# Macaron block on one NeuronCore: counts by one scan, other last groups, quarters in two steps, first loads in another order

## The chip, the core and the metric

The kernel runs on one NeuronCore of a Trainium2 chip. The time is the device time of one execution in microseconds. The figure for the kernel before is the median of three runs. Profiles are one execution each, taken by the hardware profiler; in their rows PE is TensorE, PEld its weight loads, DVE is VectorE, ACT is ScalarE, POOL is GpSimd and SP is SyncE, which issues most DMAs.

## What is computed

A block of three residual layers on x of 8 x 1024 rows of 512 numbers (fp32): half a mixture of experts, attention, half a mixture of experts with the same weights.

```python
def moe(x):                                   # T = 8192 tokens, E = 32, C = 320
    logits = xt @ w_router
    probs = softmax(logits); top1 = argmax(probs); gate = probs[top1]
    pos = cumsum(onehot(top1))[t, top1] - 1   # a token's place in its expert's queue
    accepted = pos < C
    slot = where(accepted, top1 * C + pos, E * C)
    buf[slot] = xt
    y = (silu(buf @ w_gate) * (buf @ w_up)) @ w_down
    out_tok = where(accepted, y[slot] * gate, 0)
    return xt + out_tok

x = x + 0.5 * moe(layernorm(x))
x = x + attention(layernorm(x))               # 16 heads of 32, rotary positions
x = x + 0.5 * moe(layernorm(x))
```

## The kernel before, in words

**Stages.** The front (`front`) normalizes all 64 tiles of 128 rows, computes their router logits and gives each token its slot. The first expert stage (`experts`) gathers each expert's rows, multiplies them and writes first_rows. Attention (`Attention`) reads first_rows, writes x2, and in the course of its own work routes the rows for the third layer. The second expert stage writes the output. The instructions of TensorE, ScalarE, VectorE and GpSimd stand in the order in which the Python code emits them, one queue for each engine, and each instruction waits by semaphores for what it needs. SP's queue is put in order by the scheduler of the framework.

**The front.** A loop over tiles (line 423) runs four things at different distances: it loads four tiles at a time (L373), takes the statistics of tile i + 12 on VectorE (L156, L157), normalizes tile i + 2 on ScalarE (L177), transposes tile i on TensorE (L199) and copies the transposed tile into xT (L429). Behind these, generators stand in a list `work`, and `advance` (line 410) runs each of them once per tile up to its next WAIT:

- `scaled` works out the scales of a group of tiles from its statistics. VectorE adds epsilon (L167), POOL raises to -0.5 (L168), and VectorE derives three more rows (L170 to L172).
- `products` turns four tiles' xT into logits: the router products (L234), a copy (L241), a fold (L246), a copy to lg (L251).
- `routed` runs `route` for one group, and waits until the group ahead of it has counted.

The groups have 4, six times 8, and three times 4 tiles (line 361).

**route.** For a group of G tiles it finds each token's largest logit (L285 to L294), writes oh, the one-hot rows as [128, G, 32] (L295), and counts: run holds, for each tile and expert, how many tokens of the earlier tiles went there. run begins with a copy of the carry (L299), and G adds follow, each reading what the one ahead of it wrote (L301). Two products then sum, for each token, the tokens ahead of it in its own tile and those of the tiles ahead (L306, L310). L316 picks the token's own expert out of them; from that come pos (L324), slot (L338) and spare (L343). For each tile POOL issues one indirect DMA (L347) that scatters 128 pairs of token number and gate into the table. The last group's counts go to `sorted` (line 454), which ranks the experts by size: a product (L465), some steps of VectorE, a second product (L479) and the numbers `order` and `arm` (L487 to L492). SP reads order and loads the first expert's weights, 3 MB (L509); all engines read arm and branch to one of four profiles of widths.

**The expert stage.** `places` loads the whole table into slots (L580) and turns it into indices by two small products (L584): the first gives come (which rows to gather, L586) and ids (L587), the second the gates (L587); go (L588, L591) is derived from ids. `gather` (L670) issues three indirect DMAs on POOL for an expert's rows. `begin` normalizes and transposes the first expert's rows. Then, for each of 32 experts, `feed` runs the products gate and up (L755), and down (L797, L805), while it prepares the next one; the expert after that is gathered meanwhile. Experts whose last block has at most 32 rows compute it in quarters; `quarters` (line 599) gives them their own indices: a copy of the table's rows four times over (L610), two products (L618), and come, go and gates from them (L622 to L629). It is called once, ahead of step r = 2.

**The opening of attention.** `opening` (line 1150) loads two weight tiles wqk (L1231, from `load_qk`), the first four tiles of rows xt, the tables cos and sin, and four more tiles of rows (L1164); it takes the statistics and scales tile by tile, transposes, and begins the products pq (L1258). From there TensorE works through scores, exponentials and sums in stages. `finished` (line 1514) normalizes four tiles of the new rows at a time and routes them with the same `route`, in groups of four; the last two groups come behind the last products (L1495).

Of the kernel before, what the change touches and what calls it, by code (L numbers as in the profile page):

```python
# [13 lines left out]
F32 = mybir.dt.float32  # L14
# [3 lines left out]
ALU = mybir.AluOpType  # L18
# [32 lines left out]
class Block:  # L51
# [31 lines left out]
    def constants(self, pool, w_router):  # L83
        nc = self.nc
        self.ident = pool.tile([P, P], F32, name="ident")
        make_identity(nc, self.ident)

        self.before = pool.tile([P, P], F32, name="before")
        make_upper_triangular(nc, self.before, val=1.0, diag=False)
        self.ones = pool.tile([P, P], F32, name="ones")  # L90
        nc.vector.memset(self.ones, 1.0)

        self.rev = pool.tile([P, G, self.E], F32, name="rev")
        nc.gpsimd.iota(
            self.rev, pattern=[[0, G], [-1, self.E]], base=self.E, channel_multiplier=0,
            allow_small_or_imprecise_dtypes=True,
        )

        self.token = pool.tile([P, self.NT], F32, name="token")
        nc.gpsimd.iota(  # L100
            self.token, pattern=[[P, self.NT]], base=0, channel_multiplier=1,
            allow_small_or_imprecise_dtypes=True,
        )
        self.w_router = pool.tile([P, self.KD, self.E], F32, name="w_router")
        nc.sync.dma_start(self.w_router, w_router.rearrange("(k p) e -> p k e", p=P))

        self.fold = pool.tile([P, self.E], F32, name="fold")
        nc.vector.tensor_copy(self.fold, self.ident[:, 0 : self.E])
        for k in range(1, P // self.E):
            nc.vector.tensor_tensor(  # L110
                self.fold, self.fold, self.ident[:, k * self.E : (k + 1) * self.E], ALU.add
            )
        self.power = pool.tile([P, G], F32, name="power")
        nc.vector.memset(self.power, -0.5)

        NS, E, NB = self.NS, self.E, self.NB
        self.past, self.away, self.beyond = (
            pool.tile([P, self.NT], F32, name=name) for name in ("past", "away", "beyond")
        )
        for t, add in (  # L120
            (self.past, NS), (self.away, NS - E * P), (self.beyond, -self.T)
        ):
            nc.vector.tensor_scalar(t, self.token, float(add), None, ALU.add)

        R = NB * E
        self.own = pool.tile([R, E], F32, name="own")
        self.columns = pool.tile([R, R], F32, name="columns")
        self.number = pool.tile([E, 1], F32, name="number")  # L130
        nc.gpsimd.memset(self.columns, -1.0)
        for i in range(NB):
            at = slice(i * E, (i + 1) * E)
            nc.vector.tensor_copy(self.own[at, :], self.ident[at, at])
            nc.vector.tensor_scalar(
                self.columns[at, at], self.rev[at, 0, :], -1.0, float(E), ALU.mult, ALU.add
            )
        nc.gpsimd.iota(
            self.number, pattern=[[0, 1]], base=0, channel_multiplier=1,
            allow_small_or_imprecise_dtypes=True,  # L140
        )
        self.most = pool.tile([1, len(self.profiles) - 1, E], F32, name="most")
        for j, widths in enumerate(self.profiles[:-1]):
            for a, z, width in sorted_steps(widths):
                nc.gpsimd.memset(
                    self.most[:, j, a:z],
                    float((width if width < self.C else self.T) * E + E),
                )

        self.acts = [pool.tile([P, self.KF, self.C], F32, name=f"a{i}") for i in range(2)]  # L150
        for t in self.acts:
            nc.gpsimd.memset(t, 0.0)
# [101 lines left out]
    def route(  # L254
# [22 lines left out]
            return x.unsqueeze(2).to_broadcast([P, G, E])  # L277

        token = self.token[:, t0 : t0 + G]
        ex, oh = wide("ex"), wide("oh")  # L280
        mx, se, m = narrow("mx"), narrow("se"), narrow("m")

        row = pool.tile([P, G, 2], F32, tag="row", bufs=deep, name="row")
# [11 lines left out]
        nc.vector.tensor_tensor(oh, rev, over_e(m), ALU.is_equal)  # L295


        run = pool.tile([P, G + 1, E], F32, tag="run", bufs=2, name="run")
        nc.vector.tensor_copy(run[:, 0, :], carry)  # L299
        for j in range(G):  # L300
            nc.vector.tensor_tensor(run[:, j + 1, :], run[:, j, :], oh[:, j, :], ALU.add)  # L301
        order = counted and counted(run[:, G, :])
        yield WAIT, 1
        yield PE, 1.2
        pp = psum.tile([P, G, E], F32, tag=tag, name="pp")
        nc.tensor.matmul(  # L306
            pp.rearrange("p g e -> p (g e)"), self.before,
            oh.rearrange("p g e -> p (g e)"), start=True, stop=False,
        )
        nc.tensor.matmul(  # L310
            pp.rearrange("p g e -> p (g e)"), self.ones,
            run[:, 0:G, :].rearrange("p g e -> p (g e)"), start=False, stop=True,
        )
        if apart:
            yield WAIT, 1
        nc.vector.tensor_tensor(lg, pp, oh, ALU.mult)  # L316
        yield DVE, 1.2
        nc.vector.tensor_reduce(se, ex, AX.X, ALU.add)
        nc.vector.reciprocal(se, se)
# [24 lines left out]
        for j in range(G):  # L344
# [5 lines left out]
                in_=row[:, j, :],  # L350
                in_offset=None,
            )
        return run[:, G, :]

    def front(self, pool, psum, x, rest, spare, carry, table, ranked):

# [1 line left out]


        nc, NT, D, KD, E = self.nc, self.NT, self.D, self.KD, self.E  # L360
        sizes = [G // 2] + [G] * (NT // G - 2) + [G // 2] * 3
        starts = [sum(sizes[:i]) for i in range(len(sizes))]
        group = [g for g, size in enumerate(sizes) for _ in range(size)]
        mv = pool.tile([P, NT, 2], F32, name="mv", bufs=1)
# [148 lines left out]
    def experts(self, table, ranks, src, dst, weights, loaded=None, others=None):  # L513
# [16 lines left out]
        for i in tc.Switch(which, len(self.profiles)):  # L530
            widths = self.profiles[i]
            with (
# [3 lines left out]
                tc.manual_schedule(engines={F.PE, F.Activation, F.DVE, F.Pool}),  # L536
            ):
                expert = Expert(self, (wp, ap, ps), src, views, others)
                expert.places(table, matrix)


                now = expert.gather(0, widths[0])
                now.weights = loaded or self.load(wp, order, 0, weights, hold="wu")
                expert.begin(now)
                following = expert.gather(1, widths[1])
                for r in range(E):
                    if r == 2:
                        expert.quarters(widths)
                    if following:
                        following.weights = self.load(  # L550
                            wp, order, r + 1, weights, hold=None if r else "wg"
# [7 lines left out]
class Expert:  # L559
# [7 lines left out]
    def places(self, table, matrix):  # L567
# [14 lines left out]
        for i, at in enumerate((ids, self.gates)):  # L582
            pt = self.ps.tile([P, R], F32, tag="tp", name="pt")
            nc.tensor.matmul(pt, rows[:, :, i], matrix, start=True, stop=True)  # L584
            if i == 0:
                nc.vector.tensor_scalar(self.come, pt, float(s.T - 1), None, ALU.min)  # L586
            nc.vector.tensor_copy(at, pt)  # L587
        nc.vector.tensor_copy(self.go[:, 0 : R - E], ids[:, 0 : R - E])  # L588
        for i in range(2):
# [9 lines left out]
    def quarters(self, widths):  # L599
# [3 lines left out]
        few = [r for r, width in enumerate(widths) if self.parts(width) == 4]  # L603
        if not few:
            return
        assert few == list(range(few[0], few[-1] + 1)) and few[0] > 3
        last = slice(R - E, R)
        at = slice(R - E + few[0], R - E + few[-1] + 1)
        rows = ap.tile([R, 4, n * 2], F32, tag="four", bufs=1, name="four")
# [3 lines left out]
            .to_broadcast([E, 4, n * 2]),  # L613
        )
        rows = rows.rearrange("r k (s c) -> r (k s) c", c=2)
        for i in range(2):
            pt = self.ps.tile([P, len(few)], F32, tag="tp", name="pt")
            nc.tensor.matmul(  # L618
# [203 lines left out]
class Attention:  # L822
# [327 lines left out]
    def opening(self):  # L1150
# [1 line left out]


        nc, s, pool, psum = self.nc, self.s, self.pool, self.psum
        self.load_qk(0, 0)

        def fetch(half):
            xs = []
# [7 lines left out]
            return xs  # L1166

        xs = [fetch(0)]
        nc.sync.dma_start(self.cs, self.cos)
        nc.sync.dma_start(self.sn, self.sin)  # L1170
        xs.append(fetch(1))
# [526 lines left out]
```

## Time and profile before

| | us |
|---|---|
| median of three runs (4716.10 to 4721.66) | 4720.27 |
| the profiled execution | 4731.47 |
| its span, first to last instruction | 4729.7 |
| front, to the issue of slots (L580) | 0 to 171.8 |
| first expert stage, to the last scatter of its rows | 171.8 to 935.8 |
| attention, to the issue of slots in front of the second stage | 938.3 to 3955.6 |
| second expert stage | 3955.6 to 4729.7 |

The page gives the busy time of each engine over the span: PE 4519.9 us, DVE 2827.4, ACT 2939.7, POOL 789.1. TensorE's granted clock has a mean of 0.979 of full speed.

A line of the timeline gives the start in us, the busy time in us, engine, source line, operation, out<-in by the program's names with partitions x elements, how many instructions were merged (x8), and in brackets the idle time of the engine ahead of it with the instruction that ended it, as far as the profile can tell. Lines of stretches of time give the length, then for PE, PEld, DVE, ACT and POOL the busy us and the number of instructions, then TensorE's granted clock, the share of the DMA engines and GB/s. SPq lines are DMAs that SP issues.

### The profile page before, as it was taken

The page shows a single profiled execution, that of the slowest core. Times are in us where ns is not written, and L with a number is a line of the kernel's source. Part 1 is how long each engine was busy: PE and PEld are TensorE (multiplying, and loading weights), DVE is VectorE, ACT ScalarE, POOL GpSimd, SP SyncE. Part 2 cuts the span into 40 slices and gives each one's busy share as a digit, 9 for nine tenths or more (in the row PEclk, how much of TensorE's full clock was granted, in tenths as well). Part 3 has the DMA queues.
Part 4 walks back from the last instruction along what each step waited for, and adds up shares of the span by engine and source line. Part 5 has one row for each costly group of instructions (what it writes and reads, how often), then busy time and mean ns, then how long its engine had stood idle before and what let it go on. Part 6 is the DMA issues. An engine that isn't in the chain of part 4 may idle for free.

```text
span 4729.7 us, 69515 instructions
## 1 busy us (share of the span) xinstructions
PE 4519.9 (96%) x24896; PEld 2111.9 (45%) x24896; DVE 2827.4 (60%) x5604; ACT 2939.7 (62%) x5886; POOL 789.1 (17%) x806
## 2 busy tenths in 40 slices
PE   6699999898999999999999999999999986999999
PEld 4466777632233333333333333333333324667777
DVE  8434433367667767767777777777776754344333
ACT  6212222169998888888888888888888872111111
POOL 4433333210000000010110110110110002222221
PEclk8799999989999999999999999999999998999999
DMA  4456666511112212212212212212211104455564
GB/s 145 139 185 194 208 208 230 186 56 35 34 32 61 75 37 68 69 41 67 71 40 69 68 44 63 70 44 63 72 46 54 59 26 157 167 172 190 181 207 140
DMA packets 287642, 481.60 MB, mean 102 GB/s; under 512 B 47000, under 2 KB 82274, under 8 KB 287282
## 3 DMA queue, kind: packets, MB, share of 16 engines
q1 hardware_dynamic: 253042, 400.43, 27.3%
q0 software_dynamic: 33952, 76.41, 5.1%
q8 instruction: 198, 3.24, 0.3%
q14 instruction: 162, 1.33, 0.1%
q10 hardware_dynamic: 288, 0.20, 0.0%
HBM read 376.18 MB, written 88.01 MB: 98 GB/s over the span
## 4 chain that ended last, share of the span: by engine, by line
PE 83%; DVE 7%; ACT 4%; issue 3%; DMA 2%; POOL 1%; SPq 0%; DVEq 0%; POOLq 0%; ACTq 0%
PE sa L1379 14%; PE gp L755 10%; PE pq L1258 9%; PE up L755 9%; PE po L1461 9%; PE yp L797 9%; PE sb L1359 6%; PE px L1495 4%; PE pv L1329 4%; PE sb L1386 3%; ACT junk L1398 2%; DVE nm L1394 2%; PE tp L199 2%; PE tp L743 1%; ACT pr L1391 1%
## 5 line engine op out<-in xcount | busy, mean ns | idle before, releaser
L1394 DVE TENSOR_REDUCE nm<-sa 128x2 f32<-128x1024 f32 x1024 | 1248.5, 1220 | 648.5 <-PE sa L1379 387.3
L1398 ACT ACTIVATE junk<-sa,nm 128x512 f32<-128x512 f32 x2048 | 1407.2, 687 | 264.8 <-DVE nm L1394 185.7
L1379 PE MATMUL sa<-k,q 32*128 32x512 f32 x4096 | 1147.5, 642 | 9.7 <-ACT pr L1391 3.5
L1391 ACT ACTIVATE pr<-sb 128x1024 f32<-128x1024 f32 x1024 | 1040.6, 1018 | 108.7 <-PE sb L1386 104.4
L1386 PE MATMUL sb<-q,k 32*128 32x512 f32 x4096 | 1063.9, 603 | 0.0
L760 ACT ACTIVATE sg<-gp 128x320 f32<-128x320 f32 (+7 forms) x256 | 99.5, 389 | 1108.5 <-PE gp L755 1081.1
L1309 POOL TENSOR_TENSOR raw<-raw,a 128x512 f32<-128x512 f32 x126 | 160.6, 1274 | 2367.9 <-DMA rot<-raw 1673.2
L1461 PE MATMUL po<-pr,v 128*32 128x512 f32 x4096 | 549.6, 609 | 0.0
L755 PE MATMUL gp<-bT,wg 128*128 128x272 f32 (+7 forms) x2048 | 510.2, 392 | 0.0
L1258 PE MATMUL pq<-hT,wqk 128*128 128x512 f32 x1024 | 506.7, 619 | 1.0 <-DVE hT L1199 0.8
L755 PE MATMUL up<-bT,wu 128*128 128x272 f32 (+7 forms) x2048 | 503.5, 389 | 0.0
L797 PE MATMUL yp<-wd,a 128*128 128x512 f32 x1024 | 460.3, 592 | 0.0
L1359 PE MATMUL sb<-mrow,ones 3*128 3x512 bf16 x2048 | 393.8, 385 | 41.7 <-ACT pr L1391 40.2
L755 PEld LDWEIGHTS gp<-bT,wg 128*128 128x128 f32 x2048 | 385.2, 191 | 93.9 <-issue 22.6
L755 PEld LDWEIGHTS up<-bT,wu 128*128 128x128 f32 x2048 | 386.6, 190 | 75.4
L1359 PEld LDWEIGHTS <-ones 3*128 3x128 bf16 x2048 | 99.9, 91 | 712.1 <-issue 670.4
L780 DVE TENSOR_TENSOR a<-sg,up 128x320 f32<-128x320 f32 (+7 forms) x256 | 110.6, 432 | 495.1 <-PE up L755 469.0
L1398 ACT ACTIVATION_READ_ACCUMULATOR junk<-sa,nm 128x1 f32 x2048 | 398.2, 194 | 0.0
L1386 PEld LDWEIGHTS sb<-q,k 32*128 32x128 f32 x4096 | 360.4, 184 | 0.1
L1379 PEld LDWEIGHTS sa<-k,q 32*128 32x128 f32 x4096 | 304.8, 183 | 70.3 <-ACT pr L1391 30.2
L1258 PEld LDWEIGHTS pq<-hT,wqk 128*128 128x128 f32 x1024 | 174.8, 189 | 315.8 <-issue 227.0
L801 DVE SCALAR_TENSOR_TENSOR ys<-yp,gates,x 128x512 f32<-128x512 f32 x128 | 96.1, 751 | 337.0 <-PE yp L797 337.0
(199 smaller groups left out, 4222.4 us busy)
## 6 DMA issues: line engine op xcount, KB each, us to landing
wg<-in_w_gate SPq DMA_DIRECT2D x64, 1024.0 KB
wu<-in_w_up SPq DMA_DIRECT2D x64, 1024.0 KB
wd<-in_w_down SPq DMA_DIRECT2D x64, 1024.0 KB
rot<-raw SPq DMA_DIRECT2D x1008, 32.0 KB
all<-in_x SPq DMA_DIRECT2D x32, 512.0 KB
xt<-first_rows SPq DMA_DIRECT2D x64, 256.0 KB
xr<-first_rows SPq DMA_DIRECT2D x64, 256.0 KB
d<-inverse SPq DMA_DIRECT2D x256, 64.0 KB
```

The lines of the kernel that those rows point to most:

```text
L755: nc.tensor.matmul(acc, w[:, k, f * P : (f + 1) * P], to.bT[:, k, 0:width], start=(k == 0), stop=(k == s.KD - 1),)
L797: nc.tensor.matmul(yp, a[:, f, i * P : (i + 1) * P], wd[:, f, :], start=(f == 0), stop=(f == KF - 1),)
L1258: nc.tensor.matmul(acc, w[:, which, k, :], self.hT[b, n][:, k, :], start=(k == 0), stop=(k == KD - 1),)
L1329: nc.tensor.matmul(acc, hT[:, k, at : at + P], self.w_vo[:, k, :], start=(k == 0), stop=(k == KD - 1),)
L1359: nc.tensor.matmul(sb[:, h, :], self.ones16[at : at + 3, :], row[at : at + 3, :], start=True, stop=False,)
L1379: nc.tensor.matmul(sa[:, h, :], qa[at, (g * 4 + j) * P : (g * 4 + j + 1) * P], ka[at, m * 512 : (m + 1) * 512], start=True, stop=True,)
L1386: nc.tensor.matmul(sb[:, h, :], k[at, t * P : (t + 1) * P], q[at, n * 512 : (n + 1) * 512], start=False, stop=True,)
L1391: nc.scalar.activation(pr, sb, AF.Exp)
L1394: nc.vector.tensor_reduce(nm[:, m, j, pair : pair + 2], sa, AX.X, ALU.max, negate=True)
L1398: nc.scalar.activation(self.junk, sa[:, h - pair, :], AF.Exp, bias=nm[:, m, j, h : h + 1], accum_out=se[:, m, j, h : h + 1],)
L1461: nc.tensor.matmul(self.po[at : at + HD, :], self.v[b][t][:, c * P + at : c * P + at + HD], prs[h // 2 * 2][:, h % 2, :], start=(t == 0), ...
L1495: nc.tensor.matmul(acc, self.oT[b, c, half][:, j * P : (j + 1) * P], self.w_vo[:, c, :], start=False, stop=(c == KD - 1),)
```

## The change

- `route` counts by one instruction. oh becomes a view of a tile `taken` of [128, 32, G + 1]: for each expert one column for the carry and then G columns for the tiles. A scan runs over all 32 x (G + 1) elements: each result is the one before it times `going`, plus `taken`. going is a constant with 0 in each expert's first column and 1 elsewhere, so that the sum starts anew with each expert's carry. run, pp and the operands of the two products take the same layout, with the experts outside and the tiles inside; L295 writes oh, and L316 reads pp and oh, through views with the two dimensions exchanged. The tiles going are filled on POOL at the start.
- The groups of the front have 4, seven times 8, and 4 tiles.
- `places` stops behind come; the first expert's gather is emitted there, and the rest of `places` follows.
- `quarters` stops behind its copy. The copy is emitted ahead of step 1, the products and indices ahead of step 3.
- In `opening`, load_qk stands behind the first four tiles of rows.

```diff
--- before.py
+++ after.py
@@ -110,6 +110,12 @@
             nc.vector.tensor_tensor(
                 self.fold, self.fold, self.ident[:, k * self.E : (k + 1) * self.E], ALU.add
             )
+
+        self.going = {}
+        for n in (G // 2, G):
+            self.going[n] = t = pool.tile([P, self.E, n + 1], F32, name=f"going{n}")
+            nc.gpsimd.memset(t, 1.0)
+            nc.gpsimd.memset(t[:, :, 0:1], 0.0)
         self.power = pool.tile([P, G], F32, name="power")
         nc.vector.memset(self.power, -0.5)
 
@@ -277,7 +283,12 @@
             return x.unsqueeze(2).to_broadcast([P, G, E])
 
         token = self.token[:, t0 : t0 + G]
-        ex, oh = wide("ex"), wide("oh")
+        ex = wide("ex")
+
+        taken = pool.tile(
+            [P, E, G + 1], F32, tag=f"oh{G}", bufs=2 if apart else 1, name="oh"
+        )
+        oh = taken[:, :, 1 : G + 1].rearrange("p e g -> p g e")
         mx, se, m = narrow("mx"), narrow("se"), narrow("m")
 
         row = pool.tile([P, G, 2], F32, tag="row", bufs=deep, name="row")
@@ -295,25 +306,24 @@
         nc.vector.tensor_tensor(oh, rev, over_e(m), ALU.is_equal)
 
 
-        run = pool.tile([P, G + 1, E], F32, tag="run", bufs=2, name="run")
-        nc.vector.tensor_copy(run[:, 0, :], carry)
-        for j in range(G):
-            nc.vector.tensor_tensor(run[:, j + 1, :], run[:, j, :], oh[:, j, :], ALU.add)
-        order = counted and counted(run[:, G, :])
+        run = pool.tile([P, E, G + 1], F32, tag=f"run{G}", bufs=2, name="run")
+        nc.vector.tensor_copy(taken[:, :, 0], carry)
+        nc.vector.tensor_tensor_scan(
+            run.rearrange("p e g -> p (e g)"),
+            self.going[G].rearrange("p e g -> p (e g)"),
+            taken.rearrange("p e g -> p (e g)"), 0.0, ALU.mult, ALU.add,
+        )
+        order = counted and counted(run[:, :, G])
         yield WAIT, 1
         yield PE, 1.2
-        pp = psum.tile([P, G, E], F32, tag=tag, name="pp")
+        pp = psum.tile([P, E, G], F32, tag=tag, name="pp")
         nc.tensor.matmul(
-            pp.rearrange("p g e -> p (g e)"), self.before,
-            oh.rearrange("p g e -> p (g e)"), start=True, stop=False,
-        )
-        nc.tensor.matmul(
-            pp.rearrange("p g e -> p (g e)"), self.ones,
-            run[:, 0:G, :].rearrange("p g e -> p (g e)"), start=False, stop=True,
-        )
+            pp, self.before, taken[:, :, 1 : G + 1], start=True, stop=False,
+        )
+        nc.tensor.matmul(pp, self.ones, run[:, :, 0:G], start=False, stop=True)
         if apart:
             yield WAIT, 1
-        nc.vector.tensor_tensor(lg, pp, oh, ALU.mult)
+        nc.vector.tensor_tensor(lg, pp.rearrange("p e g -> p g e"), oh, ALU.mult)
         yield DVE, 1.2
         nc.vector.tensor_reduce(se, ex, AX.X, ALU.add)
         nc.vector.reciprocal(se, se)
@@ -350,7 +360,7 @@
                 in_=row[:, j, :],
                 in_offset=None,
             )
-        return run[:, G, :]
+        return run[:, :, G]
 
     def front(self, pool, psum, x, rest, spare, carry, table, ranked):
 
@@ -358,7 +368,7 @@
 
 
         nc, NT, D, KD, E = self.nc, self.NT, self.D, self.KD, self.E
-        sizes = [G // 2] + [G] * (NT // G - 2) + [G // 2] * 3
+        sizes = [G // 2] + [G] * (NT // G - 1) + [G // 2]
         starts = [sum(sizes[:i]) for i in range(len(sizes))]
         group = [g for g, size in enumerate(sizes) for _ in range(size)]
         mv = pool.tile([P, NT, 2], F32, name="mv", bufs=1)
@@ -536,16 +546,19 @@
                 tc.manual_schedule(engines={F.PE, F.Activation, F.DVE, F.Pool}),
             ):
                 expert = Expert(self, (wp, ap, ps), src, views, others)
-                expert.places(table, matrix)
+                places = expert.places(table, matrix)
+                next(places)
 
 
                 now = expert.gather(0, widths[0])
+                next(places, None)
                 now.weights = loaded or self.load(wp, order, 0, weights, hold="wu")
                 expert.begin(now)
                 following = expert.gather(1, widths[1])
+                quarters = expert.quarters(widths)
                 for r in range(E):
-                    if r == 2:
-                        expert.quarters(widths)
+                    if r in (1, 3):
+                        next(quarters, None)
                     if following:
                         following.weights = self.load(
                             wp, order, r + 1, weights, hold=None if r else "wg"
@@ -584,6 +597,7 @@
             nc.tensor.matmul(pt, rows[:, :, i], matrix, start=True, stop=True)
             if i == 0:
                 nc.vector.tensor_scalar(self.come, pt, float(s.T - 1), None, ALU.min)
+                yield
             nc.vector.tensor_copy(at, pt)
         nc.vector.tensor_copy(self.go[:, 0 : R - E], ids[:, 0 : R - E])
         for i in range(2):
@@ -603,7 +617,7 @@
         few = [r for r, width in enumerate(widths) if self.parts(width) == 4]
         if not few:
             return
-        assert few == list(range(few[0], few[-1] + 1)) and few[0] > 3
+        assert few == list(range(few[0], few[-1] + 1)) and few[0] > 4
         last = slice(R - E, R)
         at = slice(R - E + few[0], R - E + few[-1] + 1)
         rows = ap.tile([R, 4, n * 2], F32, tag="four", bufs=1, name="four")
@@ -613,6 +627,7 @@
             .to_broadcast([E, 4, n * 2]),
         )
         rows = rows.rearrange("r k (s c) -> r (k s) c", c=2)
+        yield
         for i in range(2):
             pt = self.ps.tile([P, len(few)], F32, tag="tp", name="pt")
             nc.tensor.matmul(
@@ -1152,7 +1167,6 @@
 
 
         nc, s, pool, psum = self.nc, self.s, self.pool, self.psum
-        self.load_qk(0, 0)
 
         def fetch(half):
             xs = []
@@ -1166,6 +1180,7 @@
             return xs
 
         xs = [fetch(0)]
+        self.load_qk(0, 0)
         nc.sync.dma_start(self.cs, self.cos)
         nc.sync.dma_start(self.sn, self.sin)
         xs.append(fetch(1))
```

## The prediction

> **What bounds the kernel now.** I read the page first: the busy rows and the chain of waits. The chain is TensorE for 83 % of the span, and nothing in the change removes or shortens a large product. So the change can only move the seams: the front (0 to 172 us), the first steps of each expert stage, and the opening of attention.
>
> ```profile
> PE 83%; DVE 7%; ACT 4%; issue 3%; DMA 2%; POOL 1%; SPq 0%; DVEq 0%; POOLq 0%; ACTq 0%
> ```
>
> Then the busy time by stretches, and the timeline of VectorE, in the front. From 28 to 113 us VectorE paces it: it is busy 17 to 18 of every 20 us, and one group of eight tiles takes 15.76 us (spare at 70.20, the next at 85.96) with one idle stretch of 0.73. ScalarE has 14.5 and POOL 12.8 busy in the same 20.
>
> ```profile
> 60.00:80.00 20.00, 13.65 (x82) 8.81 (x82) 17.96 (x64) 14.50 (x29) 12.75 (x13) 0.83 0.55 150
> 79.16 0.42 DVE L295 TENSOR_TENSOR oh<-rev,m 128x256 f32<-128x256 f32 x1
> 79.50 0.17 DVE L299 COPY run<-run 128x32 f32<-128x32 f32 x1
> 79.71 1.77 DVE L301 TENSOR_TENSOR run<-run,oh 128x32 f32<-128x32 f32 x8
> 81.40 0.69 DVE L156 BATCH_NORM_STATS2 st<-xq 128x6 f32<-128x512 f32 x1
> ```
>
> Behind 113 us the timeline shows another regime. POOL issues one scatter each 1.27 us, and VectorE waits on things that had ended.
>
> ```profile
> 125.06 0.59 PE L310 MATMUL pp<-run,ones 128*128 128x256 f32 x2
> 130.13 0.42 DVE L316 TENSOR_TENSOR lg<-pp,oh 128x256 f32<-128x256 f32 x1 [5.11 <-PE tp L199]
> 146.17 0.29 DVE L316 TENSOR_TENSOR lg<-pp,oh 128x128 f32<-128x128 f32 x1 [3.51 <-remote]
> 160.25 0.39 SPq L509 DMA_DIRECT2D wg<-in_w_gate  x1
> 165.67 0.97 POOL L347 DMA_INDIRECT table<-row,slot  x1 [0.30 <-issue]
> 171.77 0.36 SPq L580 DMA_DIRECT2D slots<-table  x1
> ```
>
> The product that L316 reads ends at 125.65 and at 143.28; VectorE starts 4.5 and 2.9 us later. From 149 to 156 its small steps also lag: from mx to slot the last group takes 12.6 us, where the same twelve rows in front of the second expert stage (3939.6 to 3948.2) take 8.6. That is 4.5 + 2.9 + 4.0 = 11.4 us of stalls, found almost nowhere else in the trace, and the profiled execution (4731.47: span 4729.7 and 1.8 around it) is 11.2 above the median. I take the stalls to belong to the profiled execution. The sum below is made in its times with these stalls taken out, which is the median's frame (4720.27).
>
> **Counts by one scan.** Per group of eight it removes the eight adds: 81.40 - 79.71 = 1.69 us of VectorE's queue. It adds one scan over 32 x 9 = 288 elements. The nearest row is a two-operand pass over 256 elements (L290: 61.81, next start 62.15, so 0.34); as such a pass the scan costs 0.38. [...] No row here is a scan; I take 0.68, and the saving is 1.01. [...] oh is now written, and pp and oh are read, in steps of 8 or 9 words where they were contiguous. [...] No row of this trace has such a step; I take 0.27 each. [...] Five such groups lie in front of the slot numbers of 118.6, so 2.35; the first group of four gains 0.1 (0.79 for adds, less 0.41 for a scan of 160 and 0.27). The copy of the carry stays. TensorE's moving operand and the counts become strided too; no row shows that. I take nothing: VectorE does two statistics steps (1.6 us) between the adds and L316, while the four passes take about 0.9, which leaves 0.3 to 0.7 of cover. [...] The new memsets on POOL (some 0.7 us by the 0.2 of a 128 x 128 one) end before POOL's first power at 8.35.
>
> **Groups of eight and four.** Tiles 52 to 59 become one group. In the statistics this removes one short stall and one set of scales (0.78) and lengthens the other power from 1.04 to 1.67 (0.55): 0.2 gained. Front up to 113 us: 2.35 + 0.1 + 0.2 = 2.65 us (ends 0.3 and 5.5).
>
> The tail, with the stalls out. Before: slots of tiles 44 to 51 at 128.9; scatters fill POOL to 149.3; the last group's VectorE work starts at 141.6, the expert order comes 7.2 later at 148.8, its slots at 150.2, its last scatter ends 155.5. The 3 MB of weights that SP issues at the order hold the table back: their copying runs until about 170 in the profile, 10 us from issue, and slots goes out 171.77 - 160.25 = 11.5 after them; in front of the second stage, with no such load, it goes out 2.3 after the last scatter. So before: 149.0 + 11.5 = 160.5. After: the merged group waits for the logits of 56 to 59 (130.9), takes 3.6 to its counts, waits for its product behind the logits of 60 to 63 on TensorE (at half clock, to 136.4), has slots at 139.9, and POOL, free at 139.1, is slot-bound by 0.8; last scatter 155.3. The last group starts at 139.9 and has its order 0.3 sooner in itself, at 146.7: slots at 146.9 + 11.5 = 158.4. The gain is 2.1 us, all of it through the earlier order (ends: -2, if the merged slots come late, and 8).
>
> **First gather behind its rows' numbers.** Worth nothing. The label on the first gather names later writers, but in the second stage it starts before the go step has ended:
>
> ```profile
> 3959.04 0.26 DVE L586 TENSOR_SCALAR come<-pt 128x96 int32<-128x96 f32 x1 [1.06 <-PE pt L584]
> 3959.86 0.36 DVE L591 TENSOR_SCALAR go<-ids 64x32 int32<-64x32 f32 x2
> 3960.17 0.99 POOL L670 DMA_INDIRECT x<-x,come  x1 [6.95 <-DVE gates L587]
> ```
>
> come ends 3959.30 and the gather starts 0.87 later; in the first stage 175.53 and 0.93. The same delay with different work behind it is POOL's own start; it already waits for come alone, and the split leaves the order on each engine as it was. If I am wrong, 0.6 a stage.
>
> **Quarters in two steps.**
>
> ```profile
> 243.58 0.28 DVE L610 COPY four<-slots 32x256 f32<-32x256 f32 x1
> 244.01 0.61 PE L618 MATMUL pt<-matrix,four 32*128 32x11 f32 x4 [0.99 <-DVE four L610]
> 244.54 2.42 PE L755 MATMUL gp<-bT,wg 128*128 128x320 f32 x8
> ```
>
> TensorE stands 0.99 for the copy, in both stages (again at 4029.18). One step earlier the copy lies ahead of the product: 2 x 0.99 = 2.0 us. The copy, 0.28, now precedes the statistics of step 1; there the same lead of 1.9 us in step 2 made the following product of VectorE 0.4 late without TensorE stopping, so it is covered. The products themselves (0.53) stay, in step 3.
>
> **Rows ahead of wqk in the opening.**
>
> ```profile
> 938.32 0.38 SPq L1231 DMA_DIRECT2D wqk<-in_wqT  x1
> 939.30 4.24 SPq L1164 DMA_DIRECT2D xt<-first_rows  x8
> 944.31 0.69 DVE L156 BATCH_NORM_STATS2 st<-xt 128x6 f32<-128x512 f32 x1 [8.57 <-DMA xt<-first_rows]
> ```
>
> SP issues two wqk loads as soon as the last row has landed; the rows go out 0.98 later and queue behind 0.5 MB in pieces of 512 bytes, which the DMA engines copy from 939.0 to 942. With the rows first the first tile has an empty queue: issue 938.32, and 2.9 us for 256 KB (the first wqk load, as large, took 938.32 to 941.25), so 941.3 where it was 944.3: 3.0 us. VectorE then takes one tile each 1.26 us, slower than SP's issue of 0.47. wqk would be issued at about 940.3 and land by 945; the first pq, now 954.30, wants it at 951.3. SP's other loads behind it (the second four rows) are used at 951 too and issued no later than now. Ends: 0, if SP's queue keeps its order (cos and sin show that it isn't the order of the text), and 3.3. TensorE runs without a pause from there, so the gain is kept.
>
> **Last routes of attention.** Two groups of four on the chain (3929.0 and 3941.6): 0.38 and 0.53 less for the scans, 0.13 more for each oh and the last L316: 0.5. The other fourteen lie beside TensorE's products: nothing.
>
> Sum: 2.65 + 2.1 + 0 + 2.0 + 3.0 + 0.5 = 10.25 us; 4720.27 - 10.25 = 4710.0.
>
> **Rivals.** [...] (2) The stalls are in every run. Then the front's end comes at 171.8 also without the profiler, and merging takes one whole pass of VectorE (some 6 us) off a chain that is VectorE's: order at 150 to 157, slots at 162 to 169, a gain of 3 to 10 in place of 2.1: 4702 to 4709, middle 4706. (3) Slower: the merged group starves POOL. Half of its scatters could go out at 139.1 and now wait for eight tiles' slots. From slots at 140.2 on, each us late is one us of the end. It would need more than 10 us to lose against the rest; stalls like those of this profile, 11.4 us, laid on this one chain in every run would do: 4721 to 4735. For it: the chain has three TensorE products at half clock in it. Against it: it has 0.8 us of wait at present.
>
> **Chances.** The sum 0.43 (4707 to 4713); rival 1 0.22; rival 2 0.21; rival 3 0.14. A measurement here tells about 0.2 % from no change, 9.4 us: the bounds are 4710.8 and 4729.7. Faster: 0.27 of the sum's 0.43, 0.21 of rival 2, 0.04 of rival 1, together 0.52. Slower: 0.10 of rival 3. Same: 0.38. The range goes from 4700, below rival 2's middle, to 4721.
>
> **What would show it.** L301 gone and one scan of 0.4 or 0.7 us; L295 and L316 at 0.4 (no price for steps) or 0.7 to 0.8; 15.3 us a group. POOL without gaps over 1 us from 119 to the last scatter; slots 11.5 behind the first weight load. come to gather still 0.9. The 0.99 in front of pt gone. xt issued at once behind the last scatter, its first statistics 3.4 us behind the issue. I am wrong if the group's period doesn't fall, if the first gather moves against come, or if wqk is still first.

## The result, and the profile after

The changed kernel takes 4703.33 us (median of 7 runs, 4697.81 to 4708.43), beside it the kernel before 4719.71 (7 runs, 4716.1 to 4722.59): 16.4 us less, ratio 0.9964 with a 95% interval of 0.9954 to 0.9974. The forecast was 4710.0, range 4700 to 4721. Measured again in a later set of runs, in which the kernel before took 4729.61, it was 4717.51: 12.1 less, ratio 0.9975 (0.9965 to 0.9984).

The profiled execution took 4708.43, its span 4706.6; before it was 4731.47 and 4729.7. Between the two spans lie 23.1 us, so some 7 us of that difference isn't the change's.

The shares of the chain of waits, changed kernel:

```profile
PE 84%; DVE 6%; ACT 4%; issue 3%; DMA 2%; POOL 1%; SPq 1%; DVEq 0%; POOLq 0%; ACTq 0%
```

TensorE carries nearly the same part of the span as before (83 %). The seams moved. The table shows which: each length is from one landmark of the trace, on SP or TensorE, to the next.

| stretch | before | changed | less | forecast |
|---|---|---|---|---|
| front: start to the slots load | 171.77 | 156.34 | 15.4 | 4.75 (stalls of 11.4 taken out) |
| first expert stage: slots to SP's first issue of the opening | 766.55 | 765.71 | 0.8 | 1.0 |
| opening: first issue to first pq | 15.98 | 12.96 | 3.0 | 3.0 |
| attention: first pq to the second slots load | 3001.25 | 2998.32 | 2.9 | 0.5 |
| second expert stage: slots to the end | 774.15 | 773.27 | 0.9 | 1.0 |

Busy times from 60 to 80 us, and VectorE's queue there (start, us, engine, line, operation):

```profile
60.00:80.00 20.00, 14.23 (x83) 9.29 (x84) 18.26 (x56) 15.15 (x30) 13.13 (x14) 0.80 0.52 139
77.99 0.62 DVE L306 TENSOR_TENSOR oh<-rev,m 128x256 f32<-128x256 f32 x1
78.45 0.24 DVE L310 COPY oh<-run 128x32 f32<-128x32 f32 x1
78.72 0.76 DVE L311 TENSOR_TENSOR_SCAN run<-going,oh 128x288 f32<-128x288 f32 x1
79.40 0.67 DVE L162 BATCH_NORM_STATS2 st<-xq 128x6 f32<-128x512 f32 x1
80.99 0.57 DVE L326 TENSOR_TENSOR lg<-pp,oh 128x256 f32<-128x256 f32 x1
81.49 0.41 DVE L328 TENSOR_REDUCE se<-ex 128x8 f32<-128x256 f32 x1
```

The price of a pass in the queue is the time from its start to the start of the next. The scan takes 79.40 - 78.72 = 0.68 where eight adds took 1.69. oh takes 78.45 - 77.99 = 0.46 (0.34 before), and L326 81.49 - 80.99 = 0.50 (0.31 to 0.34 before as L316). VectorE's busy sum in the stretch hasn't fallen, because more tiles pass in it: a group takes 15.11 us (first scatters at 54.07, 69.18, 84.29), before 15.76.

The tail of the front. POOL's row of scatters, SP's loads and VectorE's L326:

```profile
116.25 1.03 POOL L357 DMA_INDIRECT table<-row,slot  x1 [4.17 <-DVE spare L353]
151.46 0.97 POOL L357 DMA_INDIRECT table<-row,slot  x1 [0.30 <-issue]
```

```profile
121.58 0.62 DVE L326 TENSOR_TENSOR lg<-pp,oh 128x256 f32<-128x256 f32 x1 [0.96 <-PE pp L323]
130.34 0.60 DVE L326 TENSOR_TENSOR lg<-pp,oh 128x256 f32<-128x256 f32 x1 [0.79 <-PE pp L323]
```

```profile
140.75 0.39 SPq L519 DMA_DIRECT2D wg<-in_w_gate  x1
156.34 0.36 SPq L593 DMA_DIRECT2D slots<-table  x1
```

The waits at L326 are 0.8 to 1.0 where the profile before had 3.5 and 5.1. From 116.25 POOL issues 28 scatters in a row with no gap over 0.30. The first weights go out at 140.75 (before 160.25), and slots follows 15.6 behind them (before 11.5) and 3.9 behind the end of the last scatter (151.46 + 0.97). So the weights no longer set slots alone; the row of scatters, which now ends later against them, is the likely cause, but no run tests it.

The first gather, second stage:

```profile
3936.83 0.26 DVE L599 TENSOR_SCALAR come<-pt 128x96 int32<-128x96 f32 x1 [1.06 <-PE pt L597]
3937.66 0.36 DVE L605 TENSOR_SCALAR go<-ids 64x32 int32<-64x32 f32 x2
...
3937.96 0.98 POOL L685 DMA_INDIRECT x<-x,come  x1 [6.41 <-DVE gates L601]
```

come ends at 3937.09 and the gather starts 0.87 later, to the hundredth as before; in the first stage it is 0.93, as before. The quarters' products, step 3 of the first stage, and the opening on SP and VectorE:

```profile
255.40 0.63 PE L633 MATMUL pt<-matrix,four 32*128 32x11 f32 x4
255.97 2.42 PE L770 MATMUL gp<-bT,wg 128*128 128x320 f32 x8
```

```profile
922.05 1.76 SPq L1178 DMA_DIRECT2D xt<-first_rows  x4
923.85 0.43 SPq L1246 DMA_DIRECT2D wqk<-in_wqT  x1
924.33 0.51 SPq L1246 DMA_DIRECT2D wqk<-in_wkT  x1
924.88 1.93 SPq L1178 DMA_DIRECT2D xt<-first_rows  x4
...
925.01 0.69 DVE L162 BATCH_NORM_STATS2 st<-xt 128x6 f32<-128x512 f32 x1 [5.34 <-DMA xt<-first_rows]
```

The product pt has no wait of its own in front of it (0.99 before). The rows go out first, and their first statistics start 2.96 behind the issue; before it was 5.99 behind the first issue (944.31 - 938.32).

### The profile page after: what moved, and what is told of

Its sections match the earlier page's. It is cut to its first block, busy times and chain, and to the rows that moved or that the text cites. A ratio compares the mean times of both kernels' runs of the same rounds, so it can differ in the third digit from the quotient of the medians.

```text
span 4706.6 us, 69374 instructions
## 1 busy us (share of the span) xinstructions
PE 4514.3 (96%) x24892; PEld 2108.6 (45%) x24892; DVE 2814.5 (60%) x5475; ACT 2939.3 (62%) x5885; POOL 791.7 (17%) x809
## 4 chain that ended last, share of the span: by engine, by line
PE 84%; DVE 6%; ACT 4%; issue 3%; DMA 2%; POOL 1%; SPq 1%; DVEq 0%; POOLq 0%; ACTq 0%
PE sa L1394 14%; PE gp L770 10%; PE up L770 9%; PE po L1476 9%; PE pq L1273 9%; PE yp L812 9%; PE sb L1374 6%; PE pv L1344 4%; PE px L1510 4%; PE sb L1401 3%; ACT junk L1413 2%; DVE nm L1409 2%; PE tp L205 2%; PE tp L758 1%; ACT pr L1406 1%
```

## The experiments

The runs came in three sets, each with the full kernel before beside it: 4719.0 us in the first set, 4730.24 in the second, 4729.61 in the third. "The first comparison" is the one above, with 4719.71.

A difference of 2 us is 0.04 % here, less than the spread of the full kernel's runs. So the front was cut out: in the four kernels of the first set all work behind the first gather is left out (no experts, no attention; a few rows are written, so that the loads stay). Their whole time is the front and some 18 us, and the four runs of each lie within 1.0 to 2.3 us.

**The front alone, before and changed.** The cut, the same in both:

```diff
-                expert.begin(now)
-                following = expert.gather(1, widths[1])
...
+                nc.sync.dma_start(dst[0:P, :], now.x[:, 0, :])
...
-    attention.run()
-    s.experts(tables[1], attention.ranks, x2, of, weights)
```

> The kernel before with all work behind the front's slot numbers and first gather left out (no experts, no attention; a few rows are written so that the loads stay). Its whole time is the front, so a stall of 11 us can't hide in the spread of 4720. Theory A (as predicted: the 11.4 us of stalls at L316 and from 149 to 156 belong to the profiled execution): the timed runs lie about 11 us below this kernel's own profiled run, near 168 to 170. Theory B (the stalls are in every run): timed runs within 2 us of the profiled one, near 179 to 182.

> The changed kernel cut in the same way. Theory A: 4.75 us below the timed runs of the cut kernel before (2.65 of VectorE, 2.1 of the tail). Theory B: 10 to 15 below, as the two profiles' slots (171.8 and 156.3) lie 15.4 apart. Theory C (A holds for the stalls, but the tail was mis-sized, since the changed trace has POOL without a gap from 116 to 152): 5 to 8 below.

Measured: before 179.76 (179.35 to 180.32), changed 172.96 (172.31 to 173.82): 6.80 less. SP's loads in the cut kernel before, and in the cut changed kernel:

```profile
149.24 0.39 SPq L509 DMA_DIRECT2D wg<-in_w_gate  x1
162.19 0.35 SPq L573 DMA_DIRECT2D slots<-table  x1
```

```profile
140.19 0.39 SPq L519 DMA_DIRECT2D wg<-in_w_gate  x1
154.79 0.35 SPq L585 DMA_DIRECT2D slots<-table  x1
```

In the cut kernel before the stalls aren't there: slots goes out at 162.19, not 171.77, and the first weights at 149.24 where the prediction worked out 149.0 with the stalls taken out. So the same work runs without the stalls. But the profiled run (179.9) isn't 11 above the other three either: it had no stall, and neither had they. "The stalls belong to the profiled execution" was the wrong name; they belong to some executions and not to others, and theory C, a mis-sized tail, fits the gain.

**Each half of the front's change.** New sizes in the kernel before, with the adds; and the scan with the old sizes:

```diff
-        sizes = [G // 2] + [G] * (NT // G - 2) + [G // 2] * 3
+        sizes = [G // 2] + [G] * (NT // G - 1) + [G // 2]
```

> The cut kernel before with the new group sizes alone (last groups of eight and four, adds kept). Theory A: 1 to 2 us below the cut kernel before. Theory B: 6 to 10 below, most of the front's gain. Theory C: 2 to 4 below.

> The cut changed kernel with the old group sizes (scan kept, last three groups of four). Theory A: 3 us below the cut kernel before (2.65 less 0.2 for the sizes, and 0.3 to 0.6 of the tail). Theory B: 4 to 6 below. Theory C: 3 to 5 below.

Measured: sizes alone 175.46 (174.29 to 175.88), 4.3 less; scan alone 175.66 (174.27 to 176.6), 4.1 less; both together 6.8. Part of the two single gains is the start: from kernel to kernel VectorE's first maximum of logits comes between 28.7 and 30.9 us, before anything of the change can act. So the landmarks of the four profiles are given from that maximum on:

| cut kernel | first maximum | slots of tiles 36 to 43 | first weights | last scatter ends | slots load | of it behind weights | behind scatter |
|---|---|---|---|---|---|---|---|
| before | 30.94 | 87.7 | 118.3 | 124.7 | 131.2 | 12.9 | 6.6 |
| sizes | 28.72 | 87.3 | 115.0 | 122.9 | 127.9 | 13.0 | 5.0 |
| scan | 30.39 | 85.8 | 114.9 | 121.4 | 128.2 | 13.3 | 6.8 |
| both | 30.38 | 84.6 | 109.8 | 120.5 | 124.4 | 14.6 | 3.9 |

Read so, sizes give 3.3 (theory C), the scan 3.0 (theory A and C), both 6.8 (theory C). Up to the slots of tiles 36 to 43 the sizes give 0.4 and the scan 1.9; the rest comes behind. In three kernels slots goes out 12.9 to 13.3 behind the first weights. With both parts it is 14.6: 1.5 us of the earlier order are lost. Here the scatters end 10.7 behind the first weights, later than in the other three (6.4 to 8.0), and the share of the DMA engines is down to 0.07 from 152 to 154, ahead of slots at 154.79. So most of the weights have landed by then, which fits a wait for the last scatter. But this is argued, not tested, and 3.9 behind the scatter isn't a fixed delay: with the copies moved to ScalarE (below) slots goes out 2.6 behind it, and 12.9 behind the first weights.

**The opening undone.** wqk is loaded ahead of the rows again:

```diff
+        self.load_qk(0, 0)
         def fetch(half):
...
         xs = [fetch(0)]
-        self.load_qk(0, 0)
```

> The changed kernel with one part undone: the first wqk loads are issued ahead of attention's first four rows again. Theory A (the sum's 3.0 us): in its profile the first statistics come 5 to 6 us behind the first issue, pq 16.0 behind it, and the run is 3.0 us above the changed kernel. Theory B (part of it is lost again, since the first oT of the changed profile is only 1.9 us nearer to the first issue than before): 1.9 above by the first oT. Theory C: the opening is where the unexplained gain lies, 5 us or more. For attention as a whole, which went from 3001.3 us (first pq to the second stage's slots) to 2998.3: if the scan made that, it stays near 2998 here; if it is one execution's luck, anything from 2997 to 3003.

Measured in the second set (before 4730.24): 4719.4, ratio 0.9978 (0.9972 to 0.9985). Its SP queue and first statistics:

```profile
931.46 0.38 SPq L1246 DMA_DIRECT2D wqk<-in_wqT  x1
931.89 0.50 SPq L1246 DMA_DIRECT2D wqk<-in_wkT  x1
932.44 3.83 SPq L1179 DMA_DIRECT2D xt<-first_rows  x8
...
936.38 0.69 DVE L162 BATCH_NORM_STATS2 st<-xt 128x6 f32<-128x512 f32 x1 [7.22 <-DMA xt<-first_rows]
```

The wait is back: 4.92 from the first issue to the first statistics, 15.32 to pq. In the five full profiles with the rows first these are 12.91 to 13.04 to pq. The opening is worth 2.3 to 3.0 us by the traces. The times are too coarse to tell theory A from B: 4719.4 is 1.9 above the changed kernel of the third set (4717.51), and against its own set's kernel before the gain is 10.8, where the changed kernel has 12.1, with intervals that overlap. Nothing speaks for theory C's 5 us or more.

**The quarters at one time.**

```diff
-                    if r in (1, 3):
+                    if r == 2:
+                        next(quarters, None)
                         next(quarters, None)
```

> The changed kernel with the quarters' indices made at one time in step 2 again. Theory A: 2.0 us above the changed kernel, 0.99 in each expert stage, seen as TensorE standing in front of pt for the copy of four. Rival: nothing, if TensorE makes the wait good in the next product. The run should be 13 to 15 us below the kernel before by theory A, 16 by the rival.

Measured: 4717.13, ratio 0.9977 (0.9967 to 0.9987). By its time nothing can be told: it stands 0.4 below the changed kernel of the third set, 4717.51. By its trace the wait is there, in both stages:

```profile
238.83 0.28 DVE L625 COPY four<-slots 32x256 f32<-32x256 f32 x1
239.26 0.60 PE L634 MATMUL pt<-matrix,four 32*128 32x11 f32 x4 [0.99 <-DVE four L625]
...
4013.62 0.60 PE L634 MATMUL pt<-matrix,four 32*128 32x11 f32 x4 [1.00 <-DVE four L625]
```

The two expert stages took 765.97 and 774.15 here. The five full profiles with two steps (the changed kernel twice, the opening undone, the scan undone, and the longer lead below) took 764.75 to 765.71, mean 765.3, and 771.59 to 773.39, mean 772.7. That is 0.6 and 1.5, together 2.1, near the 2.0 of theory A.

**Two tries at a faster front.** Copies of xT on ScalarE alone, and one tile less of lead, both in the cut changed kernel:

```diff
-                (nc.vector.tensor_copy if t % G == G - 1 else nc.scalar.copy)(to, from_)
+                nc.scalar.copy(to, from_)
```

```diff
-        ahead, soon, late, hs = G + 4, 2, None, {}
+        ahead, soon, late, hs = G + 3, 2, None, {}
```

> The cut changed kernel with all copies of xT on ScalarE (VectorE has one in eight so far, 0.6 us of a group's 15.1). Theory C of the first runs says that the changed front is set by 28 scatters in a row, counted from the slots of tiles 36 to 43 (116), and that VectorE sets when these come: five groups by 0.6 is 3.0 us less, near 170. Rival: ScalarE becomes the bound or its copies come late (it has 14.5 of 20 us busy): no gain or a loss.

> The cut changed kernel with statistics 11 tiles ahead of the transposes in place of 12. By theory C the slots of tiles 36 to 43, and with them the row of 28 scatters, come one tile's statistics sooner (0.9 us): 172.1. Rival: the scales then come just in time or late behind POOL's power, and each group waits: up to 2 us slower.

Both missed. With the copies moved a group still takes 15.07 us (first scatters at 53.20, 68.27, 83.34), and VectorE only waits longer for POOL's power (1.32 in place of 0.71). The cut changed kernel's rows show why:

```profile
69.49 0.96 POOL L357 DMA_INDIRECT table<-row,slot  x1 [0.30 <-issue]
69.97 0.68 DVE L439 COPY xT<-tp 128x512 f32<-128x512 f32 x1
70.46 1.67 POOL L174 TENSOR_TENSOR rstd<-rstd,power 128x8 f32<-128x8 f32 x1
72.17 0.17 DVE L176 SCALAR_TENSOR_TENSOR nmr<-mv,rstd 128x8 f32<-128x8 f32 x1 [0.71 <-POOL rstd L174]
```

The power starts when POOL has issued two of the group's scatters, and VectorE's next step waits for it. The copy stands in that stretch, so without it VectorE only waits longer. The adds stood outside it. With one tile less of lead a group takes 16.8 (56.99, 73.86, 90.64). The times, 176.11 and 192.93, are of the second set and aren't set against the 172.96 of the first.

**One tile more of lead, in the full kernel**, with G + 5 in that line:

> The changed kernel with statistics 13 tiles ahead of the transposes in place of 12. The copies taken off VectorE left the period at 15.1 us and only lengthened its wait for POOL's power (0.71 to 1.32), and one tile less of lead made it 16.9: so the period is set by the loop statistics, power, scales, transposes, not by VectorE's busy time. Theory A: with one tile more the wait of 0.7 goes in each group, period 14.4; five groups by 0.7 less one tile's statistics (0.9) give 2.6 us less than the changed kernel. Rival: the statistics' delay of each route eats it: same or 1 us slower.

It missed too: 4720.18, ratio 0.9980 (0.9970 to 0.9989), 2.7 above the changed kernel of the same set, with intervals that overlap. Its wait for POOL's power didn't go (0.98), and a new one of 2.35 stands in front of L326, so a group takes 17.7. So the period is that of a loop of statistics, power, scales, transposes and routes, and of the three leads tried 12 tiles is the best. Nothing that was tried beats the changed kernel by more than the noise.

**The scan undone in the full kernel**, and the changed kernel once more. The edit of the first puts back route as it was before (run in [P, G + 1, E], a loop of adds) with the new sizes.

> The changed kernel with one part undone: eight adds and contiguous oh in place of the scan, in all three places; new sizes, quarters, opening and gather kept. Theory A: the scan is worth 2.5 us in the front (175.46 less 172.96 of the cut kernels) and 0.5 behind attention: 3.0 above the changed kernel. Theory B (the 2.9 us of attention are the scan's, through shorter routes beside TensorE's products): 5 to 6 above, and attention's length, first pq to slots, at 3001 again where the changed kernel has 2998.

> The changed kernel unaltered, with more rounds. The first comparison gave 16.4 us less (ratio 0.9964, 0.9954 to 0.9974). Theory A (the parts add up: 6.8 measured for the cut front, 3.0 opening, 2.0 quarters, 0.5 to 1 last routes): 12 to 13 us less, ratio 0.9973. Theory B (some 3 to 4 us more lie in attention, as its 2.9 in the two profiles would have it): 15 to 17 less, ratio 0.9966.

Measured in one set: scan undone 4718.06 (ratio 0.9976, 0.9967 to 0.9985), changed 4717.51 (0.9975, 0.9965 to 0.9984). The 0.55 between them settles nothing: the front's stalls differ more than that from kernel to kernel in this set (slots at 164.04 and 169.45 in the two profiles, the kernel with the scan later). Attention took 2996.98 without the scan and 2997.60 with it, so theory B of the scan falls: the 2.9 us are not its doing. The change of the whole, 12.1, is as theory A expected, but the interval (7.6 to 16.5 us) holds both.

**Whom the stalls follow.** The cut changed kernel once more, unaltered, in the third set:

> The cut changed kernel unaltered, beside full kernels of this call: it asks whom the stalls of the front's tail follow. Theory A (they follow the chip or its state, whatever the kernel): its time is near 173 if the profiles of the full kernels in this call have no stalls of 4 to 5 us on VectorE between 120 and 150, and near 180 or more if they have. Theory B (they follow the program): 173 in either case.

Measured: 185.05 (183.87 to 186.23), where the same program took 172.96 (172.31 to 173.82) in the first. The kernel before took 4729.61 in this set and 4719.0 beside the first cut kernels. The same copy on VectorE, in the first set's profile and in this one's (of the first, from the whole queue of VectorE; of the second, with TensorE's last transposes ahead of it):

```profile
124.14 0.68 DVE L439 COPY xT<-tp 128x512 f32<-128x512 f32 x1
```

```profile
121.29 1.09 PE L205 MATMUL tp<-ident,h 128*128 128x128 f32 x8
128.31 1.91 PE L252 MATMUL lp<-fold,parts 128*128 128x32 f32 x8 [5.93 <-ACT parts L247]
...
134.72 0.69 DVE L439 COPY xT<-tp 128x512 f32<-128x512 f32 x1 [10.73 <-remote]
```

By the records its transposes ended at 122.38, and VectorE began at 134.72. Theory A holds: the stalls come with the set of runs, in the changed kernel as well as in the one before; by their times all four runs of this program have them here, and none of the four there. Both sets ran under the same chip number (1; the second set under 7), so, if the number names the same chip, it isn't a matter of which chip. In the profile of the changed full kernel of this set the wait at that copy is 13.54.

## Why the prediction was right or wrong

**The scan: right, its strides too dear.** No row of the kernel before shows the forecast's 0.68 and 0.41 for the scans of 288 and 160 elements, or its 0.27 and 0.13 for a strided pass over eight and over four tiles; with them a group of eight was to gain 1.01 - 2 x 0.27 = 0.47, and five groups 2.35. In the changed kernel the scans take 0.68 and 0.41 (34.02 to 34.43). The two strided passes cost 0.46 - 0.34 and 0.50 less 0.31 to 0.34, together 0.3, where 0.54 was taken; in the last group of attention, of four tiles, they cost 0.23 - 0.21 and 0.30 - 0.21 (from 3919.75 and 3923.12). A group of eight gains 15.76 - 15.11 = 0.65, not 0.47. TensorE's strided operand, taken at nothing, shows no cost: at a granted clock of 1.00 the two products of pp take 0.60 and 0.59 in the changed kernel (120.51 and 120.94), as before (124.62 and 125.06).

**"VectorE paces it": too simple.** VectorE is busy 17 to 18 of 20 us, but taking 0.6 us of copies a group off it left the period at 15.07. VectorE's work counts where it doesn't stand beside POOL's power. The adds counted, so the gain came.

**Front up to the tail: right.** From the first maximum to the slots of tiles 36 to 43 it is 3.1 less in the cut kernels (87.7 to 84.6), for a forecast of 2.65. Alone the sizes give 0.4 (forecast 0.2) and the scan 1.9 (forecast 2.45), so 0.8 comes only with both.

**The tail: right in kind, too small.** 6.8 less 3.1 leaves 3.7 for a forecast of 2.1. Two terms of the sum were mis-sized.

The first is "slots goes out 171.77 - 160.25 = 11.5 after them ... So before: 149.0 + 11.5 = 160.5". The 11.5 is one reading, and the lowest there is: in the three cut kernels of the first set other than the changed one it is 12.9 to 13.3, in the five full profiles of the later sets 12.6 to 13.8. The cut kernel before has slots at 162.2: 1.7 later than the forecast's starting point, and so 1.7 more to gain.

The second is the earlier order. The merged group's slots were forecast at 139.9 - 2.65 = 137.3 and come at 132.9; the first weights, forecast at 146.9 - 2.65 = 144.3, go out at 140.2. The step that failed is "waits for the logits of 56 to 59 (130.9) ... waits for its product behind the logits of 60 to 63 on TensorE (at half clock, to 136.4)". Both are right for the kernel before: its cut kernel has these logits at 130.6, and TensorE done with the last ones at 136.4. But they hold for its order of instructions, in which the route of tiles 52 to 55 stands ahead of them. Two rows of the cut kernel before, and two of the changed one:

```profile
131.80 0.68 DVE L429 COPY xT<-tp 128x512 f32<-128x512 f32 x1
132.63 1.91 PE L234 MATMUL pl<-xT,w_router 128*32 128x512 f32 x8
```

```profile
124.14 0.68 DVE L439 COPY xT<-tp 128x512 f32<-128x512 f32 x1
124.96 1.06 PE L240 MATMUL pl<-xT,w_router 128*32 128x512 f32 x8 [0.79 <-DVE xT L439]
```

Before, VectorE's last copy of xT follows the adds of that route, 2.9 behind the slots of tiles 44 to 51 (spare at 128.91). With the groups merged it follows these slots at once (spare at 124.05), ahead of the route, and the products for the last logits take 1.06 in place of 1.91 (granted clock 1.00 in place of 0.50). So the merged group starts at 124.73 and takes 8.5 us, where two groups took 12.7 (128.99 to 141.69). The kernel with the new sizes alone has the same order: its merged group starts 0.8 behind the slots of tiles 44 to 51 (127.22 and 126.42).

Slots then goes out 14.6 behind the first weights, not 11.5. So the end was met by luck: 158.4 - 2.65 = 155.75 forecast, 154.8 in the cut kernel with a start 0.6 earlier. An order 4.1 too late and a wait 3.1 too short nearly cancel.

**First gather: right.** come to gather 0.87 and 0.93 in both kernels: nothing.

**Quarters: right.** Both waits of 0.99 are gone, and return when the part is undone; 2.0 forecast, 2.1 between the stages of the traces.

**Opening: right.** The rows are out first, wqk 1.8 behind (forecast 2.0), pq 3.0 sooner than before and 2.3 sooner than with the part undone.

**Last routes of attention: not seen.** From the last oT to slots it is 48.27 before, 48.54 changed, 47.50 in the changed kernel's second profile, 48.01 with the scan undone. The two profiles of the changed kernel alone differ by 1.0, so a gain of 0.5 can't be seen.

**The sum.** 6.8 + 3.0 + 2.0 is 11.8 us that the runs account for (11.1 with the opening at 2.3), beside 10.25 forecast. It agrees with the 12.1 of the third set. In the first comparison it leaves 4.6 of the 16.4, just outside the interval (12.3 to 21.7 us). What that is stays open. Attention was 2.9 shorter in the profiles; its lengths are 3001.25 and 3001.67 in the two kernels with wqk first, and 2993.58, 2993.65, 2996.98, 2997.60 and 2998.32 in the five with the rows first. That hints at the opening's order, but the times don't bear it out: undoing the order costs 1.3 to 1.9 us by them, not 3 and several more. They are too coarse to rule it out.

**The rivals.** Rival 1 stood for a gain below the sum's; the gain is above it, 16.4 and 12.1 to 10.25. The time lies in rival 2's band (4702 to 4709), but only half for its reason. That merging "takes one whole pass of VectorE ... off a chain that is VectorE's" held: the tiles 52 to 59 take 12.7 us in the cut kernel before and 9.3 with the new sizes alone (127.22 to 136.54). That the stalls are in every run did not: the cut front of the first set shows none, and in the later sets, where both kernels have them, the gain is smaller, not larger. Rival 3, a starved POOL, is refuted: the row of scatters has no gap over 0.30, and the kernel isn't slower.

## What to carry to other kernels

A time read from the profile before holds for its order of instructions. Where a change takes a step out of the queues (here one group's route), what stood behind that step can move up too: work those times out anew, on every engine (here the copy on VectorE went from 131.80 to 124.14, and the products on TensorE from 132.63 to 124.96). A wait read once is one sample: 11.5 here was the lowest of the nine above. An engine that is busy most of the time need not set the period: the 0.6 us of copies that stood in VectorE's wait for POOL cost nothing, and without them a group still took 15.07. A part worth 2 us of 4700 is priced in a kernel that is cut down to it, and in the trace's waits, not by whole times; and in each trace from a first landmark on, since the start itself differs by 2 us.

## What the runs showed of the hardware that was not expected

The same instructions can take 12 us longer in one stretch of 30 us from one set of runs to another. Up to 116 us the changed kernel is the same in both (first scatter of the last row at 116.25 and 116.20). Then, by the records, TensorE's results reach VectorE late: in the cut kernel 12.3 us behind the modelled end of the transposes (134.72 - 122.38). The cut kernel took 172.3 to 173.8 in one set and 183.9 to 186.2 in the other, under the same chip number.

In the stalled profile of the cut kernel the granted clock falls from 1.00 to 0.50 within 124 to 128, in the other within 128 to 132. The fall doesn't begin the stall. The granted clock is still 1.00 from 120 to 124 in the stalled cut kernel, where the wait begins at 122.38, and 1.00 from 124 to 128 in the kernel before, where it begins at 125.65. What else differed between the sets isn't known, so the cause stays open.
